# A separate PSUM pool for the opening stages, unread identity products in PE's waits, and two bias products moved earlier

## The chip, the cores and the metric

One core of one Trainium2 chip runs the whole program in a single launch. The metric is the device time of that launch in microseconds (us), from several executions, together with one profiled execution whose trace gives every instruction of the engines: PE (TensorE, matmuls; its weight loads are listed apart as PEld), DVE (VectorE), ACT (ScalarE), POOL (GpSimd) and SP (SyncE, which here issues most DMAs).

## What is computed

The input is x of shape 4 x 512 x 288 and a condition vector per batch element. Four blocks follow each other. The first one matters here:

```
U, _  = qr(P)                      # P: 288 x 64
R     = expm(A(silu(cond) @ W.T + b))   # A: skew-symmetric 64 x 64, one per batch element
z     = x @ U
x     = x + (z @ R - z) @ U.T
```

Then come three transformer blocks with adaptive layer norm, attention of 16 heads of 18 features over 512 tokens, and an MLP (in the third block four experts with the two best chosen). Everything is float32.

## The kernel before

**The opening.** The orthonormal basis is not formed by a library routine. A loop over the 64 columns of P (`for i in range(D)`, line 564) runs two chains together. `gram_step(i+1)` (line 398) eliminates in the Gram matrix X: PE sends row i+1 of X to all partitions (`g_bc`, a 64x64 selection times 65 columns), and DVE then makes a reciprocal `rn`, a column `Fm` and the new `X`. `sign_step(i)` (line 408) works on `Wt` in the same way from `w_bc`, with six operations of DVE that end in a new `Wt`. Both products come from `to_all` (line 393). ACT takes a square root `Nm` from `g_bc` in each column, and POOL one small product `Rh`.

Other work is threaded into the same loop by generators. `main` is `skew_and_exp` (line 422): transposes `p_WT` of the weights W, the product `p_v`, the matrix `up` through DRAM, a series `p_ser` and 16 squarings `p_sq` for the exponential. `side` is `project_P` (line 527; transposes `p_t` of x and the product `p_zP`) and then the first modulations (`p_mod`). `fills` are ACT's clearing of buffers. From line 560 on, matmuls, DVE and ACT work keep the order of the program (`keep_in_program_order`), so in each column PE's queue holds `g_bc` of the next column, `w_bc`, a piece of main, a piece of side, another piece of each, and then the next column's `g_bc`. In column 60 the loop also calls `head_biases(0)` (line 202: ten very small products `p_qkb`, two copies on ACT, one multiplication on DVE).

**The tail of the opening** (lines 590 to 607): `p_RY`, a copy by DVE, `p_MT`, a copy by DVE. Then `rotate(0)` (line 610) makes `p_EU` and the products `p_xr`, which DVE adds to x; `normalize` (line 639) makes layer norm statistics; `project(0)` (line 1029) transposes the normalised x (`p_t`), multiplies by the q, k and v weights (`p_qk`, `p_v`) and sends q and k through DRAM (`qd`) into head layout. With `rotate(1)` threaded in, `for t in range(LOOK)` (line 1290) makes the first ten row-maximum steps of attention: `maxima` (line 1104) is two products `p_s` of 32 rows and a maximum by DVE. After that `attend` runs for batch after batch, and in its first round `projection_bias(0)` (line 193: six matmul passes `p_bv`, one addition on DVE) is called before it.

[...]One pool `ps` serves the whole program: three single banks `mm` (`pmm`, line 79), two double banks `big` (`pbig`), one bank `acc` (`pacc`). `to_all` takes its tiles from `big`, so that of `g_bc` and `w_bc` two are alive at a time.

Of the kernel before, what the change touches and what calls it, by code (L numbers as in the profile page):

```python
# [9 lines left out]
F32 = mybir.dt.float32  # L10
# [4 lines left out]
PSUM = bass.MemoryType.PSUM  # L15
# [18 lines left out]
D = 64  # L34
# [13 lines left out]
def cond_seq_kernel(ctx: ExitStack, tc: tile.TileContext, a: dict, out: bass.AP):  # L48
# [16 lines left out]
    matmul, transpose = InOrder(nc.tensor).matmul, InOrder(nc.tensor).transpose  # L65
# [6 lines left out]
    wmlp = ctx.enter_context(tc.tile_pool(name="wmlp", bufs=1))  # L72
    work = ctx.enter_context(tc.tile_pool(name="work", bufs=2))
    mods = ctx.enter_context(tc.tile_pool(name="mods", bufs=1))
    ps = ctx.enter_context(tc.tile_pool(name="ps", bufs=2, space=PSUM))
    blocks = ctx.enter_context(ExitStack())
    fixed = blocks.enter_context(tc.tile_pool(name="fixed", bufs=1))

    def pmm(name):
        return ps.tile([128, 512], F32, tag="mm", name=name, bufs=3)  # L80

    def pbig(name):
        return ps.tile([128, 2, 512], F32, tag="big", name=name)

    def pacc(name):
        return ps.tile([128, 512], F32, tag="acc", name=name, bufs=1)

    def row(v):
        return v.rearrange("(o n) -> o n", o=1)

# [12 lines left out]
    ident = const.tile([128, 128], F32, name="ident")  # L105
# [87 lines left out]
    def projection_bias(l):  # L193

        wqk, wv, wp, brow, bv = WA[l]
        p = pmm(f"p_bv{l}")
        for m in range(NO):
            r = slice(0, QP if m < NO - 1 else LO)
            matmul(p[0:64, :C], bv[r, m, :], wp[r, m, :], start=(m == 0), stop=(m == NO - 1))
        vector.tensor_add(wp[0:64, NO - 1, :], wp[0:64, NO - 1, :], p[0:64, :C])  # L200

    def head_biases(l):
        QB[l] = to_columns(f"qkb{l}", WA[l][3])
        if l != 1:
            vector.tensor_mul(QB[l], QB[l], scol)
# [155 lines left out]
    with tc.tile_pool(name="l0", bufs=1) as l0, tc.tile_pool(name="l0w", bufs=2) as l0w, \  # L361
# [29 lines left out]
        Hs = l0.tile([D, D], F32, name="Hs")  # L391

        def to_all(name, i, src):
            p = pbig(name)[:D, 0, :src.shape[-1]]
            matmul(p, ident[:D, i:i + 1].to_broadcast([D, D]), src, start=True, stop=True)
            return p

        def gram_step(i):
            bc = to_all(f"g_bc{i}", i, X[:, i:i + D + 1])
# [164 lines left out]
        for i in range(D):  # L564
            column[0] = i
            if i + 1 < D:
                gram_step(i + 1)
            if i == D - 1:

                dg = l0.tile([D, 3], F32, name="dg")  # L570
                junk = l0.tile([D, D], F32, name="junk")
                vector.scalar_tensor_tensor(junk, Nm, 2.0, ident[:D, :D], ALU.mult, ALU.mult, accum_out=dg[:, 0:1])
                vector.reciprocal(dg[:, 1:2], dg[:, 0:1])
            bc = to_all(f"w_bc{i}", i, Wt[:, i:])
            beside = i >= 6 and (i < 15 or i >= 18)
            next(main, None)
            if beside:
                next(side, None)
            sign_step(i, bc)
            next(main, None)  # L580
            if beside:
                next(side, None)
            next(fills, None)
            if i == 27:

                WA.append(load_attn(0, "L1_cond_W_qkv", "L1_cond_b_qkv", "L1_cond_W_proj", "L1_cond_b_proj"))
            if i == D - 4:
                head_biases(0)
        for _ in main:
            pass  # L590
        for _ in side:
# [1 line left out]
        preload()  # L593


        vector.scalar_tensor_tensor(junk, Hs, 2.0, ident[:D, :D], ALU.mult, ALU.mult, accum_out=dg[:, 2:3])
        Y = l0.tile([D, D], F32, name="Y")
        vector.tensor_scalar(Y, X[:, D:], dg[:, 1:2], dg[:, 2:3], ALU.mult, ALU.mult)
        pt = pmm("p_RY")
        for b in range(B):  # L600
            matmul(pt[:D, b * D:(b + 1) * D], Rm[0][:, b, :], Y, start=True, stop=True)
        RY = l0.tile([D, B * D], F32, name="RY")
        vector.tensor_copy(RY, pt[:D, :B * D])
        pt = pmm("p_MT")
        for b in range(B):
            matmul(pt[:D, b * D:(b + 1) * D], RY[:, b * D:(b + 1) * D], Y, start=True, stop=True)
        vector.tensor_copy(MT, pt[:D, :B * D])


    def rotate(n):  # L610
# [402 lines left out]
    with tc.tile_pool(name="attn", bufs=2) as at:  # L1013
# [90 lines left out]
        def maxima(G, step):  # L1104

            n, g = divmod(G, NG)
            j, hp = divmod(step, 2)
            p = pbig(f"p_s{G}_{step}")
            for i in range(2):
                r = slice((2 * hp + i) * HS, (2 * hp + i + 1) * HS)  # L1110
                matmul(p[:, i, :], Q[n % 2][r, g, j * 128:(j + 1) * 128], K[n % 2][r, g, :], start=True, stop=True)
            vector.tensor_reduce(M[G % 2][:, j, 2 * hp:2 * hp + 2, HD:HD + 1], p, AX.X, ALU.max)
# [146 lines left out]
        def until_none(gen):  # L1259
            for cost in gen:  # L1260
                if cost is None:
                    return
                yield cost
# [7 lines left out]
        turn = rotate(0)  # L1271
        norm = normalize(0, 0, 0)
        next(turn)
        for _ in range(NT):
            next(turn)
            next(norm)
        for _ in norm:
            pass
        for _ in turn:
            pass  # L1280
        norm1 = normalize(0, 0, 1)
        rest = rotate(1)
        sent = False
        for cost in project(0, norm):
            next(norm1, None)
            sent = sent or cost is None
            if sent and cost == 0.95:
                next(rest, None)
        norm = norm1
        for t in range(LOOK):  # L1290
            maxima(*divmod(t, 8))
            if t == 8:
                take_maxima(0)
            next(norm, None)
            next(rest, None)
        for n in range(NB):
            l, b = divmod(n, B)
            last = n and divmod(n - 1, B)

            fill, side, total = [], [], 0.0  # L1300
            if n == 1 or n == B + 1:
                WA.append(load_attn(l + 1, *(("L2_cond_w_qkv", "L2_cond_b_qkv", "L2_cond_w_proj", "L2_cond_b_proj"),
                                             ("L3_cond_w_qkv", "L3_cond_b_qkv", "L3_cond_w_proj", "L3_cond_b_proj"))[l]))
            if n == 2 or n == B + 2:
                if l == 0:
                    center_heads(1)
            if n + 1 < NB:
                new = project(n + 1, norm)
                fill.append(until_none(new))
                total += 15.3 + (4.5 if (n + 1) // B == 1 else 0.0)  # L1310
            if n:
                load_gates(n - 1)
                inverse = invert(n - 1)
                side.append(at_steps(inverse, "..I..I.....III"))
                fill.append(finish(n - 1, inverse))
                total += 6.4
            if n + 1 < NB:
                fill.append(new)
                total += 5.7
            if n and last[0] < 2:  # L1320
                norm2 = normalize(last[0], 1, last[1], n - 1)
                side.append(norm2)
                fill.append(layernorm(last[0], 1, last[1], hT[1], norm2))
                total += 1.8
            if n == NB - 3:
                prepare_routes()
                load_mods(0)
                load_mods(1)
            for r in {NB - 2: (0, 1), NB - 1: (2,)}.get(n, ()):
                norms[r] = normalize(2, 1, r, 2 * B + r)  # L1330
                side.append(norms[r])
            if n == NB - 2:
                fill.append(routed(norms[0], 0))
                total += 18.0
            if n == NB - 1:
                fill = [routed(norms[1], 1), place(0), fill[0]]
                load_mods(2)
                total += 26.0
            if n == 0:
                fill.append(modulations(range(2, 6)))  # L1340
                total += 7.2
                projection_bias(0)
            if n + 2 < NB:
                norm = normalize((n + 2) // B, 0, (n + 2) % B)
                side.append(norm)
            if 2 <= n < 2 + 2 * NE:
                fill_table(n - 2)
            attend(n, itertools.chain(*fill), total, first_ready(side))
            if n == 2 or n == B + 2:
                projection_bias(l + 1)  # L1350
                head_biases(l + 1)
                if l == 0:
                    head_norms()
            if n == 0:
                WM.append(load_mlp(0, "L1_cond_W_fc1", "L1_cond_b_fc1", "L1_cond_W_fc2"))
            if 1 <= n <= 2 * B:
                mlp(n - 1)
            if n == B:
                WM.append(load_mlp(1, "L2_cond_w1", "L2_cond_b1", "L2_cond_w2"))
# [148 lines left out]
```

## Time and profile before

| what | us |
|---|---|
| runs shown: 2097.26, 2107.14, 2112.30; median | 2107.14 |
| the profiled execution, its own time | 2096.97 |
| its span, first to last instruction | 2095.3 |
| mean granted clock of PE | 0.950 of full |
| the column loop, from the first `rn` to the last `Hs` of DVE | 7.63 to 146.67 |
| the first `p_qk` | 164.63 |
| the first `p_s` | 186.04 |
| the first `p_st` (attention proper) | 215.53 |

PE is busy in 91% of the span, but a matmul is counted as busy until its modelled end, so that a busy row doesn't say that PE runs at its peak. The row PEclk of the page gives the clock that PE was granted, in tenths of full speed per slice; in the opening it is often 5. A matmul in float32 appears as two records. In the rows of a window table the columns are the length, the busy us (and number) of PE, PEld, DVE, ACT and POOL, then the granted clock, the share of the DMA engines and GB/s. In a list of waits they are the total us, how often, and the longest.

### The profile page before, as it was taken

To read this page: it belongs to the slowest core of one execution; us is meant where nothing else is said; L and a number is where in the kernel's file an instruction comes from. 1 tells how busy PE (TensorE), PEld (TensorE's weight loads), DVE (VectorE), ACT (ScalarE), POOL (GpSimd) and SP (SyncE) were. 2 spreads that over 40 slices of the span, in tenths; PEclk is the share of its full clock that TensorE was granted. 3 is DMA by queue.
4 is the path that set the end of the run, shared out by engine and by line. 5 is a ranking of instruction groups with operands and counts; after the bars stand their busy time and mean duration, and the time that the engine had idled before them with its cause. 6 is when DMAs were issued, how large, how long until landed. Compare 5 with 4: busy or idle time off the path is not lost. (4 is left out here: it accounts for less than half of the span.)

```text
span 2095.3 us, 26242 instructions
## 1 busy us (share of the span) xinstructions
PE 1911.5 (91%) x10269; PEld 932.4 (45%) x10269; DVE 928.8 (44%) x1953; ACT 780.4 (37%) x1169; POOL 251.6 (12%) x362
## 2 busy tenths in 40 slices
PE   6769989999999999899999999999987799999997
PEld 4544323343533434334234343343322367777775
DVE  6764536436165362462643626345576334111111
ACT  5121445434354344443543434434444322212111
POOL 1000001000011020110100000000000211332322
PEclk9576999999999999999999999999998989999999
DMA  3211144022031221511213112051212445766663
GB/s 96 70 40 46 35 98 138 19 74 60 14 76 42 65 68 45 124 52 49 69 33 74 44 50 83 20 134 34 82 45 65 152 159 180 235 187 219 199 204 95
DMA packets 89419, 187.23 MB, mean 89 GB/s; under 512 B 25453, under 2 KB 50456, under 8 KB 86802
## 3 DMA queue, kind: packets, MB, share of 16 engines
q1 hardware_dynamic: 77462, 103.39, 19.0%
q0 software_dynamic: 11248, 79.79, 11.8%
q10 hardware_dynamic: 584, 2.36, 0.3%
q8 instruction: 81, 1.33, 0.3%
q14 instruction: 44, 0.36, 0.1%
HBM read 152.49 MB, written 55.45 MB: 99 GB/s over the span
## 5 line engine op out<-in xcount | busy, mean ns | idle before, releaser
L60 ACT ACTIVATE e<-p_st 128x1024 f32<-128x1024 f32 x384 | 392.7, 1023 | 675.1 <-PE p_st L60 670.8
L60 DVE TENSOR_REDUCE store<-p_s 128x2 f32<-128x1024 f32 x384 | 470.1, 1225 | 374.4 <-PE p_st L60 331.5
L60 PE MATMUL p_s<-store 32*128 32x512 f32 x1536 | 450.8, 662 | 81.2 <-DVE store L60 78.7
L60 PE MATMUL p_st<-store 32*128 32x512 f32 x1536 | 442.4, 653 | 0.9 <-DVE store L60 0.9
L60 PEld LDWEIGHTS p_s<-store 32*128 32x128 f32 x1536 | 122.0, 188 | 312.3 <-DVE store L60 223.7
L60 PE MATMUL p_av<-e,store 128*32 128x512 f32 x1536 | 210.8, 622 | 2.0 <-ACT e L60 2.0
L60 PE MATMUL p_he<-hTe,store 128*128 128x256 f32 (+1 forms) x1026 | 200.1, 404 | 4.2 <-DVE hTe L60 4.2
L60 PE MATMUL p_ye<-store,hide 128*128 128x288 f32 x684 | 175.0, 415 | 7.1 <-ACT hide L60 7.1
L60 ACT ACTIVATE hide<-p_he,store 128x256 f32<-128x256 f32 x171 | 68.5, 471 | 281.8 <-PE p_he L60 281.8
L60 PEld LDWEIGHTS p_he<-hTe,store 128*128 128x128 f32 (+1 forms) x1026 | 147.7, 191 | 53.0 <-issue 30.5
L60 PE MATMUL p_qk<-hT,wqk 128*126 128x512 f32 (+1 forms) x360 | 163.6, 625 | 0.0
L697 POOL TENSOR_TENSOR x<-x,gated 128x288 f32<-128x288 f32 x80 | 63.6, 795 | 829.9 <-DVE gated L60 829.8
L60 PE MATMUL p_h<-hT,w 128*128 128x512 f32 (+1 forms) x432 | 157.1, 619 | 5.2 <-DVE store L60 5.2
L60 PEld LDWEIGHTS p_ye<-store,hide 128*128 128x128 f32 x684 | 130.2, 193 | 47.0 <-ACT hide L60 10.9
L60 DVE TENSOR_TENSOR gated<-p_y,gate 128x288 f32<-128x288 f32 x32 | 14.6, 457 | 287.5 <-PE p_y L60 287.5
L60 PE MATMUL p_y<-w,hid 128*128 128x288 f32 x576 | 141.8, 407 | 0.0
L60 PEld LDWEIGHTS p_y<-w,hid 128*128 128x128 f32 x576 | 108.8, 190 | 35.5 <-issue 6.1
L60 PEld LDWEIGHTS p_st<-store 32*128 32x128 f32 x1536 | 117.4, 185 | 9.4 <-issue 6.2
L60 PEld LDWEIGHTS p_h<-hT,w 128*128 128x128 f32 (+1 forms) x432 | 60.9, 189 | 99.9 <-issue 83.8
L60 PE MATMUL p_o<-wp,oc 126*128 126x288 f32 (+1 forms) x288 | 92.7, 442 | 1.3 <-DVE oc L60 1.3
L60 PEld LDWEIGHTS p_qk<-hT,wqk 128*126 128x126 f32 (+1 forms) x360 | 47.9, 179 | 98.8 <-issue 98.7
L60 DVE COPY hTe<-p_te 128x512 f32<-128x512 f32 x19 | 13.1, 690 | 172.7 <-PE p_tf L60 127.8
(248 smaller groups left out, 1730.1 us busy)
## 6 DMA issues: line engine op xcount, KB each, us to landing
store<-qd SPq DMA_DIRECT2D x96, 144.0 KB
qd<-stage SPq DMA_DIRECT2D x48, 252.0 KB
od<-o SPq DMA_DIRECT2D x192, 36.0 KB
rd<-rd SPq DMA_DIRECT2D x12, 576.0 KB
oc<-od SPq DMA_DIRECT2D x24, 252.0 KB
rb<-rd SPq DMA_DIRECT2D x24, 252.0 KB
etab<-in_L_cond_w_dram SPq DMA_DIRECT2D x4, 1296.0 KB
etab<-in_L_cond_w_dram SPq DMA_DIRECT2D x8, 576.0 KB
```

What stands on the lines that cost most here:

```text
L60: ins = f(*args, **kw)
L697: nc.gpsimd.tensor_add(x[b][:, j, :], x[b][:, j, :], t)
```

## The change

A pool `ps0` holds PSUM during the opening: four `mm` banks, two single banks `row` for the tiles of `to_all`, one `acc`, and one bank `idle`. It is closed after `p_MT`, and `ps` with its former layout is opened then. A new function `keep_warm(bank, n)` multiplies the identity by the identity, n columns wide, into a bank that nothing reads: all 128 rows and 128 columns of the array, in pieces of at most 512 columns. It is called

- at the end of every column of the loop, with 512 columns for i < 4, 128 for 4 <= i < 16 and 40 <= i < 57, and 256 elsewhere;
- with 256 after `p_RY` and after `p_MT`, and 256 after `p_EU`;
- with 1024 after the first half of `rotate(0)`, and 256 after its second half;
- with 512 twice inside `project(0)` (after q and k are sent), with 512 after it, and with 128 in each of the last five steps of LOOK.

`head_biases(0)` leaves column 60, and `projection_bias(0)` leaves the first round of attention; both go between the first half of `rotate(0)` and the 1024 columns.

```diff
+    banks = {}
     def pmm(name):
-        return ps.tile([128, 512], F32, tag="mm", name=name, bufs=3)
+        return banks["pool"].tile([128, 512], F32, tag="mm", name=name, bufs=banks["mm"])
...
+    def keep_warm(bank, n):
+
+        for c in range(0, n, 512):
+            w = min(n - c, 512)
+            matmul(bank[:, :w].rearrange("p (o m) -> p o m", m=128), ident,
+                   ident.rearrange("p (o m) -> p o m", o=1).to_broadcast([128, w // 128, 128]), start=True, stop=True)
...
+    head = ctx.enter_context(ExitStack())
+    banks.update(pool=head.enter_context(tc.tile_pool(name="ps0", bufs=2, space=PSUM)), mm=4)
...
         def to_all(name, i, src):
-            p = pbig(name)[:D, 0, :src.shape[-1]]
+            p = banks["pool"].tile([128, 512], F32, tag="row", name=name)[:D, :src.shape[-1]]
...
+        def idle_bank(name):
+            return banks["pool"].tile([128, 512], F32, tag="idle", name=f"idle_{name}", bufs=1)
...
             if beside:
                 next(side, None)
+
+            keep_warm(idle_bank(i), 512 if i < 4 else 128 if 4 <= i < 16 or 40 <= i < 57 else 256)
             next(fills, None)
...
-            if i == D - 4:
-                head_biases(0)
...
             matmul(pt[:D, b * D:(b + 1) * D], Rm[0][:, b, :], Y, start=True, stop=True)
+        keep_warm(idle, 256)
...
             matmul(pt[:D, b * D:(b + 1) * D], RY[:, b * D:(b + 1) * D], Y, start=True, stop=True)
+        keep_warm(idle, 256)
         vector.tensor_copy(MT, pt[:D, :B * D])
+    head.close()
+    banks.update(pool=ctx.enter_context(tc.tile_pool(name="ps", bufs=2, space=PSUM)), mm=3)
...
         next(turn)
+        keep_warm(pmm("idle0"), 256)
         for _ in range(NT):
             next(turn)
             next(norm)
+        head_biases(0)
+        projection_bias(0)
+        keep_warm(pmm("idle1"), 2 * 512)
         for _ in norm:
             pass
         for _ in turn:
             pass
+        keep_warm(pmm("idle2"), 256)
...
             if sent and cost == 0.95:
                 next(rest, None)
+                keep_warm(pmm("idle3"), 512)
+        keep_warm(pmm("idle4"), 512)
         norm = norm1
         for t in range(LOOK):
             maxima(*divmod(t, 8))
+            if t > 4:
+                keep_warm(pmm(f"idle5_{t}"), 128)
...
-                projection_bias(0)
```

## The prediction

> **What bounds the kernel now.** I read the page's PEclk row, then window tables over the first 218 us (the only part that the change touches), then the waits of DVE there, then the timeline of single columns.
>
> ```profile
> PEclk9576999999999999999999999999998989999999
> ```
>
> One slice is 52 us: PE has half or 0.6 to 0.7 of its clock in much of the first 210 us, and nearly all of it later. By stage:
>
> ```profile
> 51.20:72.60 21.40, 17.39 (x68) 8.92 (x68) 16.34 (x92) 4.55 (x15) 1.83 (x10) 0.50 0.62 148
> 72.60:98.10 25.50, 18.53 (x218) 16.43 (x218) 21.20 (x113) 2.01 (x12) 2.42 (x12) 0.50 0.08 21
> ...
> 136.50:147.10 10.60, 5.34 (x28) 4.50 (x28) 8.11 (x50) 2.32 (x8) 0.95 (x5) 0.50 0.00 0
> 147.10:164.60 17.50, 14.13 (x48) 8.41 (x49) 9.48 (x28) 2.25 (x5) 0.00 (x0) 0.50 0.00 1
> 164.60:186.00 21.40, 21.00 (x64) 8.88 (x62) 4.89 (x17) 7.11 (x13) 0.00 (x0) 0.94 0.34 98
> 186.00:201.40 15.40, 15.34 (x32) 6.07 (x32) 6.36 (x8) 0.00 (x0) 0.00 (x0) 0.56 0.08 18
> 201.40:215.50 14.10, 13.49 (x33) 4.26 (x30) 8.87 (x8) 0.00 (x0) 0.00 (x0) 0.50 0.00 0
> ```
>
> In the loop DVE is the busiest (21.2 of 25.5), in LOOK (186 to 215) PE is. What full clock can be worth is bounded by what DVE waits for PE, first in the loop, then in LOOK:
>
> ```profile
> DVE rn L60 <- PE g_bc L60: 13.9, 22, 1.8
> ```
> ```profile
> DVE store L60 <- PE p_s L60: 9.5, 7, 2.3
> DVE x L60 <- PE p_xr L60: 6.1, 4, 3.1
> ```
>
> So at most 14 us in the loop and some 16 in LOOK, before the new matmuls cost anything. A light column (nothing of main or side) shows DVE's own pace: `rn` to `rn` is 1.81 us at full clock (43.20 to 45.01) and 1.83 at half (68.89 to 70.72). There half clock costs nothing; it costs where a column carries PE work.
>
> **When the clock is kept.** All changes of clock in the trace lie at multiples of 3.413 us from its start (27.3, 51.2, 102.4, 116.1, 122.9, 136.5, 167.3, 187.7, 218.5). Two such windows beside a change, and one in LOOK:
>
> ```profile
> 129.70:133.10 3.40, 2.21 (x46) 1.88 (x42) 2.98 (x17) 0.99 (x4) 0.36 (x2) 1.00 0.01 2
> 133.10:136.50 3.40, 1.14 (x8) 0.75 (x8) 2.90 (x19) 1.19 (x6) 0.37 (x2) 1.00 0.00 0
> ...
> 204.80:208.20 3.40, 3.20 (x10) 1.00 (x8) 2.35 (x3) 0.00 (x0) 0.00 (x0) 0.50 0.00 0
> ```
>
> The first kept full clock, the second lost it, the third has PE busy throughout and stays at half: its `p_s` use 32 of 128 rows each. I therefore sum, per window, each record's streaming time ([...]a 512-wide record follows another after 0.427 us at full clock, 0.853 at half) times its share of the 128 rows. Over the 613 windows of the trace this parts cleanly: full clock was kept at 0.38 and above and lost at 0.36 and below; half clock was left at 0.76 and above, kept at 0.72 and below. The window 204.8 comes to 0.50: enough to keep, too little to raise.
>
> The Trainium skill (TensorE: Matmul & The Clock Gate, Part 1 and "Why this matters for your kernels") has the same window, 3413 ns, but asks for no PE gap above some 3 us. By it the short gaps of the new kernel would never lose the clock, and the 14 + 16 us would come back less the new work in front of others (some 10, below): 20 us. The row 133.10 speaks against it: there PE pauses for under 0.7 us at a time (longest wait `w_bc` 0.65) and the clock falls. I go by the row.
>
> **The change part by part.** [...]128 columns 0.213 us at full clock (0.427 at half), 256: 0.427 (0.853), 512: 0.853 (1.707). Nothing reads them, so only what stands behind them on PE waits: the next `g_bc`, then `rn` and the rest of DVE's column. The order of a column sets a limit:
>
> ```profile
> 30.24 0.60 PE L60 MATMUL p_t<-ident,x 128*96 128x128 f32 x4
> 30.77 0.33 PE L60 MATMUL g_bc<-X,ident 64*64 64x65 f32 x2
> 31.37 0.29 PE L60 MATMUL w_bc<-Wt,ident 64*64 64x54 f32 x2 [0.27 <-DVE rn L60]
> ```
>
> `w_bc` at 29.55, 0.86 us of `p_WT` and `p_t`, `g_bc` ready at 31.10, `rn` at 31.15. From `w_bc` to `g_bc` ready is 0.74 + F for other work F (1.0 + F at half clock), and `w_bc` comes 2.04 after `rn`; two columns take the sum of both, so a column takes the larger of 1.82 and (2.78 + F)/2, at half clock (3.04 + F)/2 (check: F 0.85 gives 1.95, trace 1.96, the mean of the two from 55.27 to 59.18). F up to 0.86 is free.
>
> *Loop, i < 4* (512): the clock is at half (`g_bc` 0.47 us at 14.68). Window share about 1.7/2.4 + bits = 0.8, so it rises near 13.7 instead of 27.3. Two columns at 2.4 to 2.5 instead of 1.9: -1.2 us. *Columns to 15* (128): ACT's 1.9 us clearings bound the early ones; the three columns ending at 27.5 go from 7.23 to 3 x 1.93 (F 1.07): +1.4, and +0.3 before them; seven later ones lose 0.1 to 0.15: -0.9. *i = 16 to 26* (256): `p_v` columns F 1.28, three times -0.17: -0.5; five `p_t` columns (9.68 us from 49.50 to 59.18) at 1.82: +0.6; three `p_zP` columns 7.89 us to 3 x 2.03: +1.6, less if half lost. *Light columns i = 27 to 30 and 57 to 63* (256): share (0.427 + 0.07)/1.8 = 0.28, below 0.36: the clock falls after a full window, then each costs (1.0 + 0.853 + 1.99)/2 - 1.77 = 0.15: -0.8. *`p_ser` columns* (9, now 2.13, bound by DVE): with half clock 2.43, share (0.98 + 0.853)/2.43 = 0.75, just where it rises: between 0 and -2.7, I take -1.0 (it should rise within some windows). *`p_sq` and `p_mod` columns* (128): three columns to 104.03 go from 8.28 to 6.85, +1.4; four columns to 123.47 from 11.2 to 9.1 if the clock survives the window at 112.6 (0.34 now, plus 0.06): +2.1 or -0.5, I take +1.2; the others lose 0.08 to 0.2: -0.9. *Column 60*: without `p_qkb` its 3.04 becomes 1.77: +1.3. The sum is +2.5 us, with -3 and +7 as ends.
>
> *Tail*: the clock is at half on arrival. Three times 256 (0.853) behind `p_RY`, `p_MT`, `p_EU` covers copies of 0.4 us, and each delays what follows by some 0.25: -0.75. After the fourth `p_xr` PE now does `p_qkb` (2.1 at half, row 140.05), `p_bv` (2.9 issued) and 1024 columns (3.4), before the second half's `p_xr` and before `p_t`:
>
> ```profile
> 212.26 3.33 PE L60 MATMUL p_bv<-wp,bv 126*64 126x288 f32 x6
> ```
>
> Their loads were issued at 72.8 to 74.8; neither moved step issues a DMA. POOL's clearing of the next `bv` waits for `p_bv` (70 us until 215.7 today) and now comes sooner; nobody waited for it. `p_bv` and the identity products have shares 0.75 and 1, so the clock rises about 1.2 us before the 1024 end. PE: 2.1 + 2.9 + 2.9 = 7.9, then 1.9 (`p_xr`), 0.4, and 1.6 from `p_t` to `p_qk`; against 157.24 to 164.63 now, `p_qk` comes some 6 us later, less the loop's gain; its first five records then run at full clock, +1.3. Queued behind the addition that takes `p_bv` are DVE's `rstd` and `xn`, behind the two copies ACT's `rstd`; both finish inside the 1024 columns, and if those were gone they would show. Tail: -5.5.
>
> *Project*: 3 x 0.853 lie between `p_v` and the first `p_s`, which today waits 0.44 for the DMA of q and k. -2.1.
>
> *LOOK*: `p_bv` leaves: +3.3. Today a step with `p_xr` takes 4.2 (190.82 to 195.04), one without 1.7. At full clock: maximum 1.23 + `p_s` 1.1 + hand-overs = 2.45, and 1.27 bound by DVE. Three and seven of them with the rest: 29.5 becomes about 17.6, that is +12 with `p_bv`. But the share is (0.43 + 0.48)/2.45 = 0.37 in the first three, 0.34 in the next two, then 0.50 with the 128 columns: exactly at the edge. At half clock throughout, the five 128 cost 2.1: +1.2. I take the middle, the first three steps at full clock and then half: 1.2 + 3 x 1.75 = +6.4.
>
> The pools and the fourth `mm` bank: `row` keeps two tiles alive as `big` did, all tiles of `ps0` are read by the time of `p_EU`: 0, and 0.5 each way. Nothing after 218 us changes but its start.
>
> Sum: 2.5 - 5.5 - 2.1 + 6.4 = **+1.3 us**, 2094 against the span of 2095.3 (execution 2097.0). The median shown is 10 above that execution; the four executions average 2103.4, so I place the forecast at **2102**.
>
> **Rivals.** *The clock holds through LOOK* (30%): the trace's kept windows reach down to 0.38, and a window's content varies by half a step. Then 2.5 - 5.5 - 2.1 + 12 = +7, with the loop's upper end +11: about 2094. *The clock is never held where it matters* (20%; the other side): the light columns speak for it. The mechanism is in the tail: 7.9 us of PE work in front of `p_xr` and `p_t` at half clock, which nothing hides; with LOOK at half clock 0 - 6.5 - 2.1 + 1.2 = -7.4, about 2110. It decides if the windows from 190 to 198 fall below 0.36. *The gap rule holds after all, or the loop's work counts for more than rows* (8%): +20, about 2082. *No effect beyond scatter* cannot be told from the likeliest. The likeliest has 42%, own range 2093 to 2110.
>
> **How the numbers follow.** About 1% (21 us) is what a measurement of this kernel can tell from no change. Faster by more needs the last rival or a lucky median: 0.08. Slower by more needs over 2128, beyond every case: 0.04. The range takes in the scatter of the executions shown (2097 to 2112) around +11 and -7: 2088 to 2114.
>
> **What would show it.** Right: PEclk full from about 14 to 50 us; clock falling again after the last `p_sq`, rising in the 1024 columns; `p_qk` at 165 to 169; LOOK's first steps 2.4 us, later ones 1.7 to 2.1. Wrong: full clock in the columns after the last `p_sq` (256 columns are enough), or no change at 14. If `p_st` starts before 208 LOOK held; if after 219 the tail decided.

## The result, and the profile after

| | before | after |
|---|---|---|
| median of the runs that were compared (14 each), us | 2101.31 | 2118.39 |
| profiled execution, its own time | 2096.97 | 2124.97 |
| its span | 2095.3 | 2123.2 |
| mean granted clock | 0.950 | 0.951 |

The ratio is 1.0076, with a 95% interval from 1.0048 to 1.0103: the change costs about 16 us where the forecast was 2102 with 2114 as its upper end. The two profiled executions differ by 28 us. Of these, 16.6 have arrived by the time of the first attention steps (245.31 against 228.72 for the fifth `e`, ACT's exponentials in attention), and the distance is still 15.7 at the 64th (421.25 against 405.51). Another 10.9 come between the 331st and the 384th `e`, far behind everything that the change touches. That stretch before and in the changed kernel (columns as before: length, PE, PEld, DVE, ACT, POOL, granted clock, DMA, GB/s):

```profile
1499.70:1659.10 159.40, 133.05 (x838) 47.84 (x832) 96.90 (x194) 64.78 (x77) 15.26 (x19) 0.91 0.24 70
```
```profile
1518.50:1688.70 170.20, 141.94 (x838) 50.98 (x830) 96.71 (x194) 64.70 (x77) 15.25 (x19) 0.87 0.22 66
```

It is the same work at a lower clock. In the traces of the change and of kernels 4, 5, 6, 7, 10 and 12 below, this stretch holds 34 to 38 us at half clock without a break and takes 169.4 to 170.2 us; in those of before and of kernels 1, 2, 3, 8, 9 and 11 no such run is over 18 us, and it takes 156.0 to 161.0. So these 10.9 us belong to the execution, and the 16.6 are what has to be explained. The ratios below leave out executions more than 1.5% above the fastest of their kernel: one each of kernels 5, 9 and 11, and four of the eleven of kernel 10, whose times over all eleven average 0.9995 of before.

The page's clock row of the changed kernel:

```profile
PEclk9877799999999999989999999999999699999999
```

The second to fourth slice (52 to 210 us, with holes) have 8, 7, 7 where before had 5, 7, 6. The fifth has 7 where before had 9, since LOOK now reaches into it. PE was granted more clock in the loop and the projection, and the opening became longer. The waits of DVE in the loop and then in LOOK, changed kernel (total us, times, longest):

```profile
DVE rn L60 <- PE g_bc L60: 20.1, 33, 2.2
```
```profile
DVE store L60 <- PE p_s L60: 12.3, 9, 2.2
DVE x L60 <- PE p_xr L60: 1.5, 2, 1.0
```

These are the waits that the change could shrink. The first grew from 13.9 to 20.1: these 6.2 us are nearly all of the loop's loss. In LOOK the two together fell only from 15.6 to 13.8. The windows by stage, changed kernel:

```profile
100.60:118.30 17.70, 16.03 (x219) 11.00 (x219) 11.33 (x63) 5.96 (x22) 1.28 (x7) 1.00 0.24 59
118.30:131.90 13.60, 13.44 (x113) 11.04 (x113) 7.19 (x38) 2.99 (x12) 1.93 (x7) 0.50 0.31 75
...
158.80:180.40 21.60, 20.37 (x56) 10.24 (x56) 9.54 (x29) 1.93 (x7) 0.26 (x1) 0.59 0.00 1
180.40:202.90 22.50, 22.48 (x70) 9.56 (x70) 4.80 (x15) 7.41 (x13) 0.00 (x0) 1.00 0.38 105
202.90:217.30 14.40, 13.80 (x37) 5.30 (x36) 8.22 (x8) 0.00 (x0) 0.00 (x0) 0.64 0.00 1
217.30:231.00 13.70, 13.70 (x34) 5.78 (x34) 6.82 (x6) 0.00 (x0) 0.00 (x0) 0.50 0.00 0
...
114.90:118.30 3.40, 1.96 (x26) 1.38 (x22) 1.61 (x9) 1.69 (x7) 0.18 (x1) 1.00 0.09 19
```

Read them in order of time. From 100 to 118 full clock, but PE busy 16.03 of 17.70 and DVE only 11.33: here PE is what a column waits for. The window at 114.9 came to a share of 0.36 and lost the clock, and 118 to 132 runs at half with PE busy throughout. The tail (158.8 to 180.4) is at half nearly to its end. LOOK starts at full clock (202.9), loses it at 207.0, and ends at half.

The opening in four stretches, of every kernel run here (us; the loop is the time of the 64th `rn`, the tail goes from there to the fifth `stage` of `p_qk`, the projection from there to the first `p_s`, LOOK to the first `p_st`):

| kernel | loop | tail | projection | LOOK | `p_st` at | ratio of times to before, 95% |
|---|---|---|---|---|---|---|
| before | 144.3 | 34.9 | 6.8 | 29.5 | 215.5 | |
| the change | 150.9 | 42.9 | 9.1 | 28.2 | 231.0 | 1.0076 (1.0048 to 1.0103) |
| 1: moves, no products | 142.9 | 40.1 | 6.8 | 28.0 | 217.9 | 1.0023 (0.9999 to 1.0047) |
| 2: pools only | 145.6 | 35.1 | 6.8 | 29.6 | 217.1 | 1.0004 (0.9974 to 1.0034) |
| 3: loop products only | 153.0 | 35.3 | 6.8 | 29.4 | 224.6 | 1.0038 (1.0014 to 1.0062) |
| 4: no loop products | 143.3 | 42.9 | 9.1 | 27.9 | 223.2 | 1.0030 (1.0005 to 1.0056) |
| 5: LOOK, 128 in each step | 145.4 | 34.9 | 7.4 | 21.2 | 208.8 | 0.9958 (0.9927 to 0.9988) |
| 6: the same on 32 rows | 145.2 | 34.9 | 7.3 | 30.4 | 217.7 | 0.9976 (0.9947 to 1.0004) |
| 7: loop resized | 144.7 | 34.0 | 6.9 | 29.6 | 215.2 | 1.0015 (0.9980 to 1.0051) |
| 8: resized everywhere | 144.7 | 30.4 | 7.4 | 21.0 | 203.5 | 0.9983 (0.9948 to 1.0017) |
| 9: as 8, trimmed | 144.7 | 41.2 | 7.4 | 20.9 | 214.2 | 0.9998 (0.9965 to 1.0031) |
| 10: as 8, steps moved | 145.5 | 46.3 | 7.4 | 34.2 | 233.3 | 0.9939 (0.9905 to 0.9974) |
| 11: change, no products in 40 to 56 | 146.4 | 43.5 | 9.1 | 25.4 | 224.4 | 1.0001 (0.9969 to 1.0032) |
| 12: as 10, clock raised first | 143.7 | 37.9 | 7.4 | 20.4 | 209.4 | 1.0008 (0.9973 to 1.0042) |

Kernels with the same loop (before, 2, 5, 6) differ by 1.3 us in it; that is the scatter of one trace. The ratios have intervals of 0.3% (7 us), so that single stretches are judged by the traces and the ratios only for the sum.

### The profile page after: what moved, and what is told of

It is laid out like the page before. It is cut to its first block, busy times and chain, and to the rows that moved or that the text cites. A ratio compares the mean times of both kernels' runs of the same rounds, so it can differ in the third digit from the quotient of the medians.

```text
span 2123.2 us, 26557 instructions
## 1 busy us (share of the span) xinstructions
PE 1963.8 (92%) x10425; PEld 957.5 (45%) x10425; DVE 930.3 (44%) x1953; ACT 779.9 (37%) x1169; POOL 252.0 (12%) x362
## 5 line engine op out<-in xcount | busy, mean ns | idle before, releaser
L60 PE MATMUL p_st<-store 32*128 32x512 f32 x1536 | 447.9, 662 | 0.9 <-DVE store L60 0.9
L60 PE MATMUL p_qk<-hT,wqk 128*126 128x512 f32 (+1 forms) x360 | 161.0, 617 | 0.1
L60 PEld LDWEIGHTS p_ye<-store,hide 128*128 128x128 f32 x684 | 130.3, 193 | 46.5 <-ACT hide L60 10.9
L60 PEld LDWEIGHTS p_y<-w,hid 128*128 128x128 f32 x576 | 108.9, 190 | 35.3 <-issue 6.1
L60 PE MATMUL p_o<-wp,oc 126*128 126x288 f32 (+1 forms) x288 | 100.7, 473 | 1.3 <-DVE oc L60 1.3
L60 PE MATMUL p_v<-wv,hT 128*128 128x288 f32 (+1 forms) x288 | 88.6, 443 | 0.0
```

The costliest lines, as they stand in the source:

```text
L60: ins = f(*args, **kw)
```

## The experiments

**1 to 4: which part costs.** Four partial versions of the change. Theory A: the products cost their own time on PE; B: the two moved steps cost; C: the pools cost.

Kernel 1 is the change without any call of `keep_warm`; for the loop, and in the same way elsewhere:

```diff
-            keep_warm(idle_bank(i), 512 if i < 4 else 128 if 4 <= i < 16 or 40 <= i < 57 else 256)
```

Kernel 2 is that with both steps back at their old places:

```diff
+            if i == D - 4:
+                head_biases(0)
...
-        head_biases(0)
-        projection_bias(0)
...
+                projection_bias(0)
```

Kernel 3 is kernel 2 with the change's products in the loop (the line above put back). Kernel 4 is the whole change without that line.

> The change with every identity product left out: the pools and the two moved steps stay. Theory A (the identity products' own time on PE at half clock is what costs): no more than 2 us from the kernel before; column 60 gains 1.3, p_qkb and p_bv in front of p_xr and p_t cost 4 to 5, LOOK gains 3.3. Rival B (the two moved steps cost, because nothing in the tail hides them): 8 us or more slower, p_qk late by 8 or more. Rival C (the separate pools cost): as much slower as the change itself, 16 us, with gaps of PE where tiles wait.

> Only the two pools with the fourth mm bank and the row tag; no identity products, nothing moved. Theories A and B: 0, within 3 us of the kernel before, column by column the same. Rival C: slower by most of the 16 us.

> The pools and the identity products of the column loop; none in the tail, project or LOOK, nothing moved. Theory A: slower by about 8 us, all of it within the loop (first columns 2 to 3, columns with p_ser 2, with p_sq 4 or more), and after the loop nothing comes back, since the clock has fallen before the loop ends. Rival B: 0 or faster, as the clock is full in most of the loop.

> The change without the identity products of the column loop; those of the tail, project and LOOK and the two moved steps stay. Theory A: about 8 us slower than the kernel before (tail 9, project and LOOK 0 to 2, column 60 gives 1.3 back), and together with the loop-only kernel it makes up the 16 of the change. Rival B: the whole 16.

The pools cost nothing that shows (2: ratio 1.0004, from 0.9974 to 1.0034), so C falls as the cause of 16 us. The loop's products cost 8.7 us in the trace (3: 153.0 against 144.3; 7.4 against kernel 2, which has the same pools) and 8 in the ratio, which is half of the whole; A holds for them. What is left without them (4) is 7.6 us in the trace, 6.3 in the ratio; the two halves add up to 16.3 and 14.3. The moved steps alone (1) are 2.3 us late at `p_st`, where at most 2 had been expected, and 4.8 in the ratio, whose interval begins at 0.9999. So B holds for a small part. The tail of kernel 1 (start, us, engine):

```profile
155.91 1.32 PE L60 MATMUL p_xr<-EU,hT 64*128 64x288 f32 x2 [0.64 <-DVE x L60]
157.16 2.10 PE L60 MATMUL p_qkb<-ones,brow 1*126 1x1 f32 x10
159.19 3.33 PE L60 MATMUL p_bv<-wp,bv 126*64 126x288 f32 x6
162.45 4.20 PE L60 MATMUL p_xr<-EU,hT 64*128 64x288 f32 x8
```

From `p_qkb` to the next `p_xr` 5.29 us pass at half clock, all of it in front of `p_t`. Before, `p_bv` stood between the last maximum and `p_st` (3.15 us from one to the other); without it 1.28 us of DVE's work stay there. So 1.9 come back there, not the 3.33 that `p_bv` takes, and LOOK as a whole is 1.5 shorter (its first step was 0.4 longer in this execution, 2.01 against 1.64).

**5 and 6: can the clock be held in LOOK, and by what.** Pools, then 512 columns before LOOK and 128 in each of its ten steps; nothing else. Kernel 6 is the same with a quarter of the rows.

```diff
+        keep_warm(pmm("idle4"), 512)
         norm = norm1
         for t in range(LOOK):
             maxima(*divmod(t, 8))
+            keep_warm(pmm(f"idle5_{t}"), 128)
```

And kernel 6 against 5:

```diff
-            matmul(bank[:, :w].rearrange("p (o m) -> p o m", m=128), ident,
-                   ident.rearrange("p (o m) -> p o m", o=1).to_broadcast([128, w // 128, 128]), start=True, stop=True)
+            matmul(bank[:, :w].rearrange("p (o m) -> p o m", m=128), ident[:32],
+                   ident[:32].rearrange("p (o m) -> p o m", o=1).to_broadcast([32, w // 128, 128]), start=True, stop=True)
```

> The kernel before with the new pools, 512 columns of the identity before the first p_s and 128 columns behind the first maximum of each of the ten steps of LOOK; no other products, no step moved. Theory R (each 3.413 us window is weighed by how many of the 128 rows stream; below about .37 full clock is lost, above about .75 half clock is left): p_bv at half clock and the 512 columns raise the clock near 185 us, and the steps then have a share of (.43+.48+.21)/2.45 = .46 with p_xr and .50 without, so full clock holds through all ten steps: from the first p_s to p_st about 20 to 21 us instead of 29.5, and the whole 8 to 9 us shorter than before (ratio about .996). Theory S (the products are only work, the clock in LOOK hangs on the phase of the windows): the clock falls again within one or two windows, ten products at half clock cost 4.3, and p_s to p_st takes 29 to 34 us; the whole between equal and 4 us longer.

> As the kernel with 512 columns and ten times 128 columns in LOOK alone, but each identity product uses 32 of the 128 rows, so that it takes PE the same time and does a quarter of the rows' work. Theory R (rows weigh): the share of the steps is (.43+.48+.05)/2.45 = .39 with p_xr and .37 without, and the 512 columns do not raise the clock; it stays at half or falls to it early in LOOK, p_s to p_st 29 to 34 us, the whole between equal and 4 us longer than before. Theory T (what counts is that PE has something to do, without long gaps): the same as with 128 rows, p_s to p_st about 20 us.

LOOK and two windows inside it, kernel 5 and then kernel 6:

```profile
187.67:208.83 21.16, 21.16 (x85) 9.31 (x84) 15.12 (x14) 0.00 (x0) 0.00 (x0) 1.00 0.05 11
...
195.60:199.00 3.40, 3.40 (x15) 1.32 (x14) 2.49 (x4) 0.00 (x0) 0.00 (x0) 1.00 0.02 5
```
```profile
187.33:217.74 30.41, 30.41 (x85) 12.99 (x84) 14.93 (x14) 0.00 (x0) 0.00 (x0) 0.52 0.04 8
...
195.30:198.70 3.40, 3.40 (x9) 1.50 (x7) 1.19 (x3) 0.00 (x0) 0.00 (x0) 0.50 0.02 5
```

The same number of records, PE counted as busy without a gap in both, and 21.16 us at a clock of 1.00 against 30.41 at 0.52. With all rows the shares of the windows lay between some 0.37 and 0.60; with 32 rows the first two came to some 0.28, which lost the clock, and 0.36. Theory R (a window is weighed by the rows that stream in it) holds, and T (only gaps count) falls. It also settles the rule of the Trainium skill (TensorE: Matmul & The Clock Gate, Part 1) that the prediction had set against the trace: gaps alone don't decide, since kernel 6 has none. The measurement decides here: rows count.

Kernel 5 is 0.42% faster than before (0.12% to 0.73%): ten products of 128 columns instead of five turn LOOK around. They don't do so in every execution. LOOK took 20.4 to 21.0 us with the same products in the traces of kernels 8, 9 and 12, but 34.2 in that of kernel 10. There a window began just with the first step:

```profile
199.00:202.40 3.40, 3.40 (x11) 1.55 (x10) 1.23 (x1) 0.00 (x0) 0.00 (x0) 1.00 0.37 77
```

PE is busy in all of it, but the share is some 0.32, and the clock fell at 202.4. So the phase of the windows, which theory S names, still decides there: the products leave the first step without margin.

**7: the loop with other sizes.** No products in columns 41 to 56 but 256 columns behind each second transpose of `p_mod`, and more in the light columns, which have no piece of main or side. Its loop against that of the change (the products of `p_mod` are not shown):

```diff
-            keep_warm(idle_bank(i), 512 if i < 4 else 128 if 4 <= i < 16 or 40 <= i < 57 else 256)
+            n = (128 if 6 <= i < 10 or 15 <= i < 18 or 24 <= i < 27 else 256 if 18 <= i < 24 or 32 <= i < 41
+                 else 384 if 27 <= i < 32 or i >= 57 else 0)
+            if n:
+                keep_warm(idle_bank(i), n)
```

> The kernel before with the new pools and products in the loop alone, sized by the share that a column lacks: 128 columns where the column has PE work at 6 to 9, 15 to 17 and 24 to 26, 256 at 18 to 23 and 32 to 40, 384 in the light columns 27 to 31 and 57 to 63, none elsewhere, and 256 behind each second transpose of p_mod. No tail, no LOOK, nothing moved. Theory R (the loss of the change in the loop came from sizes that leave windows below .37, so that the products run at half clock and cost twice): light columns have (.64+.07)/1.77 = .40, full clock holds from about 24 us to the end of the loop, rn 64 comes at 138 to 140 instead of 144.3 (change: 150.9), the whole 4 to 6 us shorter than before. Theory A (products in front of g_bc cost their own time whatever the clock): more columns than the change's, so rn 64 at 151 or later and the whole 6 to 9 us longer than before, as with the loop products of the change.

Half of it came: in the trace the 57th `rn` is at 128.3 (before 130.7, change 137.4), with full clock from 95 to 132. Then the light columns lost it all again. Kernel 7, 112.2 to 115.6 and the last eight columns:

```profile
128.33:144.73 16.40, 14.51 (x70) 8.67 (x70) 11.17 (x65) 2.63 (x15) 1.32 (x7) 0.63 0.01 1
112.20:115.60 3.40, 2.89 (x18) 1.67 (x17) 0.76 (x6) 2.14 (x9) 0.46 (x3) 1.00 0.09 20
```

The window at 112.2, near the one at 112.6 where before lost its clock (share 0.34), is now at some 0.52 and keeps it. The products of 384 columns began too late: the window at 129.3 still held columns without any (share 0.20), the clock fell at 132.7, and light columns with 384 at half clock then took 2.09 to 2.27 us instead of 1.77, and column 60 took 4.31 instead of 3.04. So neither number that had been expected came (138 to 140, or 151); the loop is 144.7, as before.

**8 and 9: everything resized, and trimmed.** Kernel 8 is 7 with LOOK of 5 and 256 columns behind `p_RY`, `p_MT`, `p_EU`, behind each of four `p_xr` and behind the second half of the rotation; nothing is moved. Kernel 9 leaves out what had given nothing in 8; against 8 it is:

```diff
-            n = (128 if 6 <= i < 10 or 15 <= i < 18 or 24 <= i < 27 else 256 if 18 <= i < 24 or 32 <= i < 41
-                 else 384 if 27 <= i < 32 or i >= 57 else 0)
+            n = 128 if 24 <= i < 27 else 256 if 18 <= i < 24 or 32 <= i < 41 else 384 if 27 <= i < 32 or i >= 61 else 0
```

> The resized products of the loop, plus 256 columns behind p_RY, p_MT, p_EU, behind each of the four p_xr and behind the second half of the rotation, plus 512 columns before LOOK and 128 in each of its ten steps; no step moved. Theory R: full clock from 24 us to p_st; loop 4 to 6 us shorter, the chain from p_EU to p_qk about 1 to 2 us shorter (records at full clock against 256 columns of .43 each), LOOK 8 to 9 shorter: 12 to 18 us less than before (ratio .991 to .994). Theory A or S: products cost their time in loop, tail and LOOK, the whole 8 to 15 us longer than before.

> The kernel with resized products in loop, tail and LOOK, less the products that its trace shows to have given nothing: none up to column 17 (they cost .5 there) and none in the light columns 57 to 60 (some .5 to .8). Theory R: rn 64 at 143.3 to 143.9 (before 144.3, with all resized products 144.7), full clock from about 146 on, p_st at 201.5 to 202.5 (before 215.5, all resized 203.5), the whole about 13 us shorter than before, ratio near .994. Rival: with fewer products at the end of the loop the clock is not raised before the tail, then the tail's products run at half clock, p_EU to p_qk takes 14 instead of 11.3, and p_st comes at 205 to 207.

The tail from `p_EU` to `p_qk` and LOOK, kernel 8 and then kernel 9:

```profile
150.40:161.70 11.30, 11.22 (x44) 5.87 (x44) 7.81 (x23) 1.72 (x5) 0.00 (x0) 1.00 0.00 0
182.46:203.46 21.00, 21.00 (x86) 9.31 (x85) 15.13 (x14) 0.00 (x0) 0.00 (x0) 1.00 0.04 8
```
```profile
153.05:172.60 19.55, 19.55 (x44) 10.23 (x45) 10.05 (x30) 2.20 (x5) 0.00 (x0) 0.50 0.00 0
193.25:214.16 20.91, 20.91 (x85) 9.31 (x84) 15.12 (x14) 0.00 (x0) 0.00 (x0) 1.00 0.03 6
```

The same 44 records of PE take 11.30 us at full clock and 19.55 at half. In kernel 8 the window at 142.9 (products of 384 columns, share between 0.70 and 0.77) raised the clock just before the tail. In 9 none did, which was the rival of the expectation, and the price was 8.3 us instead of the rival's 2.7: `p_st` came at 214.2, outside both forecasts. The trace of 8 reaches `p_st` 12 us earlier than before. Its ratio shows 0.17% (from 0.52% faster to 0.17% slower), less than the 0.6 to 0.9% expected. Part of the lead goes in the trace itself: it is 10.9 us at the 101st `e` and 3.7 at the 151st, and in between PE ran 20 us at half clock against 3 before.

**10 and 12: the moved steps at full clock.** Kernel 10 puts the two steps of the change into kernel 8, with 896 columns in the place of `p_qkb`. Its profiled execution is the slowest of its eleven (span 2132.5, median 2098.9), and in it the clock was lost at 147.8 and the tail ran at half, so it can't tell B1 (the steps cost their time on PE) from B2 (they cost what waits behind them on DVE and ACT). Kernel 12 puts 2048 columns before the tail to raise the clock.

Kernel 10 against 8:

```diff
-                 else 384 if 27 <= i < 32 or i >= 57 else 0)
+                 else 896 if i == 60 else 384 if 27 <= i < 32 or i >= 57 else 0)
...
-            if i == D - 4:
-                head_biases(0)
...
+        head_biases(0)
+        projection_bias(0)
         for _ in norm:
             pass
...
-                projection_bias(0)
```

Kernel 12 against 10:

```diff
-                 else 896 if i == 60 else 384 if 27 <= i < 32 or i >= 57 else 0)
+                 else 384 if 27 <= i < 32 else 0)
...
         preload()
+        keep_warm(idle_bank("end"), 2048)
```

> The kernel with resized products everywhere, with the change's two moved steps put back where the change puts them (behind the fourth p_xr); column 60 gets 896 columns of the identity instead of 384 in the place of p_qkb, so that its length and the clock stay. Theory B1 (the moved steps cost their PE time at half clock): at full clock they take 1.05 + 1.67, p_EU to p_qk goes from 11.3 to 13 to 14, LOOK gets back 1.7 by p_bv, p_st at 203.5 to 205. Theory B2 (they cost what waits behind them on DVE and ACT, whatever the clock): p_EU to p_qk goes to 17, as much more as where the two steps alone were moved at half clock (13.9 to 19.9), p_st at 206 to 208.

> The kernel with resized products everywhere and the two moved steps behind the fourth p_xr, without products in the light columns, but with 2048 columns of the identity right behind the loop: 6.8 us at half clock hold one whole 3.413 us window wherever the windows lie, so that full clock is sure before p_RY (the profile taken of the kernel with the moved steps lost it in the tail). Loop: rn 64 at 141.5 to 142.5, the 2048 columns delay p_RY by some 3 to 4. Theory B1 (the moved steps cost their PE time): p_EU to p_qk 13 to 14 us (11.3 without them at full clock, 19.9 with them at half), full clock through LOOK, p_st at 204 to 206, the whole 8 to 11 us shorter than before (ratio .995 to .996). Theory B2 (they cost what waits behind them on DVE and ACT, whatever the clock): p_EU to p_qk 17 or more, p_st at 208 or later.

Kernel 12, the end of the first half of the rotation:

```profile
160.59 0.70 PE L60 MATMUL idle<-ident 128*128 128x256 f32 x2
161.22 1.16 PE L60 MATMUL p_qkb<-ones,brow 1*126 1x1 f32 x10
162.32 1.81 PE L60 MATMUL p_bv<-wp,bv 126*64 126x288 f32 x6
164.06 2.20 PE L60 MATMUL p_xr<-EU,hT 64*128 64x288 f32 x8
```

`p_EU` to `p_qk` takes 13.5 us against 11.3 in kernel 8: 2.2 for the moved steps, whose 2.84 us (161.22 to 164.06) are PE time. By this stretch B1 holds and B2 falls. But LOOK gives back only 0.6 (20.4 against 21.0). At half clock the move is a loss: 5.2 in the tail against 1.5 in LOOK and 1.4 in column 60. At full clock it is 2.2 against 0.6; what column 60 would gain at that clock was not measured. `p_st` came at 209.4 instead of 204 to 206, because `p_EU` came 4.3 later than in kernel 8: the 64th `rn` was at 143.7 (expected 141.5 to 142.5), and from there to `p_EU`, with the 2048 columns, it took 11.0 instead of 5.7. The whole is equal to before (1.0008, expected 0.995 to 0.996).

**11: the change without its 128 columns in 40 to 56.**

```diff
-            keep_warm(idle_bank(i), 512 if i < 4 else 128 if 4 <= i < 16 or 40 <= i < 57 else 256)
+            if not 40 <= i < 57:
+                keep_warm(idle_bank(i), 512 if i < 4 else 128 if i < 16 else 256)
```

> The change as it is, without its 128 columns in columns 40 to 56 (p_sq and p_mod). Theory A (there the products cost their own time and, once the clock has fallen at 118, twice that): those columns took 36.8 us from rn 43 to rn 57 in the change and 32.6 before; without products 32 to 33, rn 64 at 146 to 147.5 instead of 150.9, everything behind it 4 us sooner, the whole 3 to 5 us shorter than the change (ratio to before 1.004 to 1.006). Theory C (the products there hold the clock up for the light columns, and cost nothing by themselves): rn 64 at 150 or later.

From the 43rd to the 57th `rn` it takes 32.3 us (before 32.6, change 36.8), and the 64th comes at 146.4: theory A (the products cost their own time) to the number, and C (they hold the clock up for the light columns) falls. The clock still fell at the same place (115.0 to 118.4, share some 0.30). At `p_st` it is 6.6 us ahead of the change, 4.4 from here; the rest is mainly LOOK, which kept full clock longer in this execution. The ratio is 1.0001 (0.9969 to 1.0032), below the 1.004 to 1.006 expected.

## Why the prediction was wrong

It forecast +1.3 us by `p_st`; the traces show -15.5. The rule of the windows held in the main, and the sum was wrong in three places: the loop by 9.1 us, LOOK by 5.1 and the tail by 2.5.

**The term that runs through all of them: the price of a product.** The prediction took streaming alone: "128 columns 0.213 us at full clock (0.427 at half), 256: 0.427 (0.853)". The traces show what a product pushes back the next instruction by. A column of the changed kernel with `p_sq` and `p_mod`, and then one at half clock:

```profile
108.60 0.66 PE L60 MATMUL p_mod<-wa,scT 96*4 96x288 f32 x6
109.19 0.49 PE L60 MATMUL idle<-ident 128*128 128x128 f32 x2
109.61 0.33 PE L60 MATMUL g_bc<-X,ident 64*64 64x65 f32 x2
...
123.05 1.21 PE L60 MATMUL p_sq<-sq 64*64 64x64 f32 x16
124.19 0.79 PE L60 MATMUL idle<-ident 128*128 128x128 f32 x2
124.91 0.47 PE L60 MATMUL g_bc<-X,ident 64*64 64x65 f32 x2
```

From start to start 0.42 at full clock and 0.72 at half; 256 take 0.63 (160.59 to 161.22 in kernel 12, above) and 1.15 (behind `p_EU` in the change), 512 at half 2.00 (first columns). Each product takes its streaming and some 0.2 (full) or 0.3 (half) more; what the rest is made of no run here separates. In kernel 11, without the product, `g_bc` starts 0.60 behind `p_mod` in such a column, here 1.01, so that the 0.42 are added in full; at half clock its columns with `p_sq` take 2.50 against 3.05. For 128 columns at full clock that doubles the price. The Trainium skill (TensorE: Matmul & The Clock Gate, Single matmul latency) puts a constant of 166 ns at full clock and 183 at half beside the streaming of a lone bf16 matmul; an estimate with this constant would have been 0.38 and 0.61 for 128 columns, near the traces at full clock and too little at half, where the traces decide.

**The loop: +2.5 forecast, -6.6 measured.** By stretches of the 64 `rn`, gain forecast and measured:

| to the `rn` | forecast | measured |
|---|---|---|
| 5th (512 columns) | -1.2 | -2.7 |
| 17th | +0.8 | +0.8 |
| 32nd (`p_t`, `p_zP`, light columns) | +1.4 | +1.4 |
| 43rd (`p_ser`) | -1.0 | -1.9 |
| 57th (`p_sq`, `p_mod`) | +1.7 | -4.2 |
| 64th (light columns, column 60) | +0.8 | +0.1 |

The rows of the 17th and the 32nd agree to the tenth by luck: their terms are off by 0.1 to 0.6 each and cancel (in the first row the later columns lost 1.3 instead of 0.9; in the second the first `p_t` column gained 0.6 that no term held, and `p_zP` gained 1.2 instead of 1.6), and kernels with the same loop differ by up to 1.1 us at the 17th `rn`.

The step that failed is "three columns to 104.03 ... +1.4; four columns to 123.47 ... I take +1.2; the others lose 0.08 to 0.2: -0.9". The first part came (6.79 us for the three, 1.1 of the gain in this row). "The others" lost 2.9. Four of them ran at full clock and lost 1.25, because a product moves `g_bc` by its whole 0.42 where the column waits for PE; beside kernel 11 the six columns to the 49th `rn` are 1.55 longer, by 0.42 in three of them and by 0.25, 0.04 and 0 in the rest. One column that ran at full clock before was now at half and lost 1.3, and the three behind it lost 0.4. And the bet on the four columns was lost: the weakest window, now at 114.9, came to 0.36 and the clock fell, so that those columns took 13.6 us with the products at half clock, against 11.2 before. The low end named for them, -0.5, was too kind by 1.9, because it left out that columns at half clock are made longer by the products. Kernel 11 shows both at once: without these products the stretch is as long as before.

The first columns have a step that the sum left out: it counted two columns, and three have a product in front of their `g_bc` at half clock. Before, and then in the change:

```profile
10.03 0.47 PE L60 MATMUL w_bc<-Wt,ident 64*64 64x64 f32 x2 [1.06 <-ACT Nm L60]
10.29 0.42 PE L60 MATMUL g_bc<-X,ident 64*64 64x65 f32 x2
```
```profile
10.10 0.47 PE L60 MATMUL w_bc<-Wt,ident 64*64 64x64 f32 x2 [1.06 <-ACT Nm L60]
10.51 2.07 PE L60 MATMUL idle<-ident 128*128 128x512 f32 x2
12.51 0.47 PE L60 MATMUL g_bc<-X,ident 64*64 64x65 f32 x2
```

This `g_bc` came 2.2 us later and its column took 1.2 more, which is most of the row's miss. The next two took 2.62 instead of 2.4 to 2.5 (the 2.00 of a 512 instead of 1.71). The clock rose at 19.3, not "near 13.7": the windows before reached some 0.53 and 0.62. The `p_ser` columns took 2.62 at half clock where 2.43 had been worked out, three of them until the clock rose, inside the bounds given.

**The tail: -5.5 forecast, -8.0 measured.** The rival that ends on the other side named this place and its price of 7.9 us. The lines of the changed kernel:

```profile
167.16 2.10 PE L60 MATMUL p_qkb<-ones,brow 1*126 1x1 f32 x10
169.19 3.33 PE L60 MATMUL p_bv<-wp,bv 126*64 126x288 f32 x6
172.45 3.78 PE L60 MATMUL idle<-ident 128*128 128x512 f32 x4
176.17 2.26 PE L60 MATMUL p_xr<-EU,hT 64*128 64x288 f32 x8
```

From 167.16 to 176.17 it is 9.0 us instead of 7.9: the clock was to rise 1.2 us before the 1024 columns end and rose with their end (176.3), so they took 3.72 instead of 2.9, and `p_bv` took 3.26 instead of 2.9. The three products of 256 cost about 2 (0.5 to 0.8 each) where 0.25 each was taken. Kernels 1 and 4 split the tail: 5.2 are the moved steps, 2.8 the products.

**The projection: -2.1 forecast, -2.3 measured.** Right, and the records of `p_qk` at full clock (180.4 to 202.9, clock 1.00) are the +1.3 forecast inside the tail's term.

**LOOK: +6.4 forecast, +1.3 measured.** The clock did what was forecast: full in the first steps, half behind. Its lines in the changed kernel:

```profile
202.88 1.13 PE L60 MATMUL p_s<-store 32*128 32x512 f32 x4
203.94 1.24 PE L60 MATMUL p_xr<-EU,hT 64*128 64x288 f32 x4
205.36 1.20 PE L60 MATMUL p_s<-store 32*128 32x512 f32 x4 [0.19 <-DVE store L60]
206.49 1.79 PE L60 MATMUL p_xr<-EU,hT 64*128 64x288 f32 x4
208.21 2.08 PE L60 MATMUL p_s<-store 32*128 32x512 f32 x4
```

The first step takes 2.48 (forecast 2.45), the second 2.85, the third 4.22 again, as the window at 203.6 came to 0.35. So two steps gained 3.1, not three 5.25. The leaving `p_bv` returned 1.5 (kernel 1, the whole of LOOK) instead of 3.3, since DVE's own 1.28 us lay beside it. The five products at half clock cost 3.5 from start to start (0.72, 0.73, 0.72, 0.59, 0.72) against the 2.1 taken. The three errors are 2.2, 1.8 and 1.4 us. From `p_st` to the fifth `e` the change lost another 1.1 us, with half clock at 231, and no term held that.

**What was right**: the windows and that rows weigh, the place of the tail's loss, and that no work behind 218 us changes but its start. Three readings were off without deciding anything. The column from 43.20 to 45.01, taken as a light one, holds `p_v`. The three `p_zP` columns give 1.8 by the sum shown, not 1.6. And the windows of before don't part cleanly: with the shares summed again, one kept full clock at 0.36 (1307.3) and one lost it at 0.40 (1430.2). The sign named for "the tail decided", `p_st` after 219, came, but the tail is only half of the loss. The base of 2103.4 was 2 us above the later median of before, so the time misses by 16 us and the sum by 17. **What the range missed**: it took the products' price as known and spread only the clock. The rival on the other side had the mechanism for the tail but the loop at 0; with the loop's own lower end, -3, it would have given -10.4, still short of -15.5, since the loop's end had been worked out with the streaming price.

**What stays open.** The ratios follow the traces only roughly: kernel 8 is 12 us ahead at `p_st` in its trace and 3.6 by its ratio, kernel 10 is 18 behind in its trace and 13 ahead by its ratio, kernel 11 is 9 behind and equal. A stretch whose windows lie near the edge goes either way: the one between the 331st and the 384th `e` does so in the 14 traces, seven to seven, and is worth some 10 us alone. That each single kernel goes both ways from one execution to the next is the likely reason, but one trace per kernel doesn't show it, and how much of the 16 us in the median comes from such stretches is not known. Kernels 5 and 10 were measured faster than before (0.4% and 0.6%). The 0.6% of kernel 10 hangs on which of its executions are counted, and for kernel 5 alone do trace and ratio say the same; one out of twelve is to be taken with care.

## What to carry to other kernels

A product that only keeps the clock up pays where PE's queue would otherwise leave the next instruction late and where it carries the stage over the edge with margin: in LOOK, ten of 128 columns turned 29.5 us into some 21 in four traces of five, while five of them, placed late, gained nothing. Price it from start to start of the next instruction, not by its streaming, and price it at half clock too, since it is at half clock that it stands when it fails: a size that misses the edge costs most. Before work is moved to fill a wait, read from the trace what lay beside it at its old place; only what is left there when it goes is given back. And before the totals of two traces are compared, look for stretches that the change doesn't touch and that ran at another clock.

## What the runs showed of the hardware

The granted clock was decided by windows of 3.413 us: in each of the 14 traces all changes of clock lie within 3 ns of multiples of it, counted from one offset per trace. The shares of some 8,600 windows were summed as in the prediction (streaming time times rows over 128, products side by side on different columns of the array counted once). No window above 0.41 lost full clock and none below 0.33 kept it; no window below 0.65 left half clock and none above 0.81 stayed there. In between both happened, so the edges are bands in this sum: 0.37 puts 45 of 7,732 windows at full clock on the wrong side, and 0.75 does so with 53 of 887 at half. The trace lacks some matmul records, so part of the width may lie in the sum.

The windows do not start with the program: counted from the start of the span they lay at 0.0 us before, 2.2 in the change, 1.0 in kernel 5 and 0.7 in kernel 6. So the same stage is cut differently in each execution, and a stage whose mean share is above the edge can still lose its clock in one window that falls on its weakest part, as at 114.9 in the change and at 199.0 in kernel 10.
